# Moving the first group's value products beside its own attention in a fused decoder layer

## The chip, the core and the metric

The kernel runs on one core of one Trainium2 chip. The metric is the device time of one execution, in microseconds (us). Five engines work side by side, each through its own instructions in order: TensorE (PE in the profile, its weight loads PEld), VectorE (DVE), ScalarE (ACT), GpSimd (POOL) and SyncE (SP), which here only issues DMA transfers. They wait for each other through semaphores. "Clock" below is the TensorE clock that the chip granted, 1.00 being full speed.

## The reference

The input x has 16 batches of 128 tokens with 512 features; a context of the same shape goes with it. One decoder layer is followed by one gated cross-attention layer, both with 16 heads of 32 features, all in 32-bit floats:

```python
qkv = layernorm(x, ln1_s, ln1_b) @ w_qkv + b_qkv            # A: self-attention
x = x + attention(q, k, v, ltor_mask) @ w_ao + b_ao
x = x + attention(layernorm(x, ln2) @ w_q + b_q, ctx @ w_kv + b_kv, cross_mask) @ w_co + b_co   # B
x = x + gelu(layernorm(x, ln3) @ w1 + b1) @ w2 + b2         # C: MLP
a = layernorm(ctx, gamma, beta)                             # D: gated cross-attention
out = x + tanh(gate) * attention(x @ Wq.T, a @ Wk.T, a @ Wv.T) @ Wo.T
```

## The kernel before

The 16 batches are four groups of four; a group has 512 tokens. The stages are A0 to A3 (self-attention of groups 0 to 3), B0 to B3 (cross-attention), C (the MLP) and D0 to D3. Activations that are multiplied by weights lie with features on the 128 partitions, as four chunks of 128 features by 512 tokens.

**Block products.** The q, k and v products of stage A are not computed as 16 plain matmuls each. `block_product` (L376) cuts the weight and the activation into 2 x 2 quarters and makes seven products of quarters, numbered 1 to 7, instead of eight, with sums of quarters made beforehand: `left_blocks` (L357) makes four sums for a weight (s3, a21 in place, s2, s4), once for all groups; `right_blocks` (L367) makes four for a group's normalized activation (t1, t2, b12 in place, t4), in tiles that all groups share (`tokens_at`). Products 1, 6 and 7 add up one after the other in PSUM bank mm0 and are copied out by ACT between; 5 and 3 add up in mm1; 2 and 4 rotate through the two pt banks. DVE adds the pieces together: these adds are put into a queue (`afterwards`) and are issued by `due()` at the start of the next step, so DVE stands behind the products of the step before.

**Attention.** `attend` (L567) goes through the sections in steps k, 16 to a section, four to a batch. A unit is four heads of one batch. At the first step of a batch PE makes its scores into the four sc banks. Each unit then goes through scaling (DVE), mask addition (POOL), minimum (DVE, one step later), four exponentials (ACT), reciprocal (DVE, two steps later) and normalization (POOL), a 32 x 32 transpose (DVE, three steps later) and a trip through DRAM, which leaves the probabilities turned (away, pT; issued by SP). Ten steps after its batch's first step come the mix with v (av, PE), and two steps on the output projection (mo, PE).

**What runs beside it.** While section i's attention runs, `jobs()` of section i + 1 hands out that section's block products by step (`BLOCKS`, L432), and `prepare(p)` of section i + 2 loads and normalizes: layer norm of one batch at p = 0, 2, 4, 6 with its transpose and its send to DRAM, the four receive DMAs at p = 9, and at p = 12 to 15 one chunk each of the turned activation (T_A, also lnT), written by ACT. Within a step the order is: scores, `due()`, the jobs, output projection, mix, `prepare`, then the units' work. All instructions are kept in program order on each engine, SP's DMA issues too.

**The start.** Section A0 has nothing before it. `begin` (L670) normalizes group 0, turns it on PE, and makes the q weight's sums on POOL. Then `attend` (L574 to L581) runs 16 steps without attention: all 21 products of A0 by `BLOCKS`, the other eight weight sums on DVE (L730), group 1's `prepare`, and the small jobs (L196 to L205): the output weight of A, the mask, gate and bias rows, the key masks, group 2's x, and the gated k weight (`gated_weight`, L1126), which is loaded in 16 small pieces and turned on DVE. With `at_start` set, the layer norm's last step is done by DVE and not by ACT. Profiles give L49 for nearly all instructions, since one helper records them; they are told apart by the names of the tiles.

Of the kernel before, what the change touches and what calls it, by code (L numbers as in the profile page):

```python
# [10 lines left out]
F32 = mybir.dt.float32  # L11
U8 = mybir.dt.uint8
AF = mybir.ActivationFunctionType
# [3 lines left out]
P = 128  # L17
# [4 lines left out]
H = 512  # L22
# [3 lines left out]
GB = 4  # L26
# [26 lines left out]
def decoder_then_gated_cross_attention(ctx: ExitStack, tc: tile.TileContext, a: dict, out: bass.AP):  # L53
    nc = InOrder(tc)
# [26 lines left out]
    def due():  # L81

        left = [do for queue in (late["dve"], late["act"]) for do in queue]
        for queue in late.values():
            queue.clear()
        for do in left:
            do()


    def load_weight(ap, r0, c0, name):  # L90

        t = wpool.tile([P, KC, H], F32, tag="w", name=name)
        nc.sync.dma_start(out=t, in_=ap[r0 : r0 + H, c0 : c0 + H].rearrange("(k p) n -> p k n", p=P))
        return t
# [14 lines left out]
    def load_batch(g, b):  # L109
        nc.sync.dma_start(out=x[g][:, b, :], in_=a["x"][g * GB + b])  # L110
# [24 lines left out]
    def load_vectors(n, engine=nc.sync, parts=slice(None)):  # L135
        row = 0
        for i, (_, ap) in enumerate(vectors[n]):
            size = ap.shape[0] // P
            if i in range(len(vectors[n]))[parts]:
                engine.dma_start(out=rows_of[n][row : row + size, :], in_=ap.rearrange("(c p) -> c p", p=P))  # L140
            row += size

    def turn_vectors(n):
        rows, (cols, _) = rows_of[n], columns[vectors[n][0][0]]
        nrow = rows.shape[0]
        tv = ps("mm", f"tv{n}")
        nc.tensor.transpose(tv[:, 0:nrow], rows, ident[0:nrow, 0:nrow])
        nc.vector.tensor_copy(cols, tv[:, 0:nrow])
# [6 lines left out]
    w = {}  # L155
# [31 lines left out]
    def key_masks():  # L187
# [5 lines left out]
        nc.tensor.transpose(tm[:, 0:NB], mrow, ident[0:NB, 0:NB])  # L193
        nc.vector.tensor_copy(mcol, tm[:, 0:NB])

    def small_jobs():  # L196
        def load_output_weight():
            w["so"] = load_weight(a["L0_xattn_w_ao"], 0, 0, "w_ao")
# [237 lines left out]
    )  # L436

    def blocks_plan(products):
        out = {}
        for jobs, steps_ in zip(products, BLOCKS):  # L440
# [126 lines left out]
    def attend(sections, ready, others, after=None):  # L567

        if not ready:
            sections[0].begin(sections[1])  # L574
            jobs = sections[0].jobs()
            for p in range(NS):
                due()
                for job in jobs.get(p, ()):
                    job()
                if p + 1 < NS:  # L580
                    sections[1].prepare(p + 1)  # L581
        at_start[0] = False
        units, batches = [], []
        projected = deque()

        def step(k, bt=None, jobs=(), ahead=None, last=True):

            m = k % GB
            pair = k - 5
            if pair % 2 and 0 <= pair < len(units):  # L590
                receive_pair(*units[pair])
            if m == 0 and bt is not None:
                scores(bt)
            due()
# [12 lines left out]
            if ahead is not None:  # L607
                ahead.prepare(k % NS)
            if 0 <= k - 3 < len(units):
                turn_unit(*units[k - 3])  # L610
            if 0 <= k - 2 < len(units):
                norm_unit(*units[k - 2])
            if 0 <= k - 1 < len(units):
                least_unit(*units[k - 1])
                exp_unit(*units[k - 1])
            if bt is not None:
                for j in SCALED[m]:
                    scale_unit(bt, j)
                bt.sec.add_mask(by_head(bt.s[m]), bt.b)

        k = 0
        for i, sec in enumerate(sections):
            last = i + 1 == len(sections)
            jobs = others() if last else sections[i + 1].jobs()
            ahead = sections[i + 2] if i + 2 < len(sections) else after if i + 2 == len(sections) else None
            for b in range(GB):
                bt = Batch(sec, b)
                batches.append(bt)
                for m in range(GB):
                    units.append((bt, m))  # L630
# [15 lines left out]
    def add_row(g, row_, b):  # L646
        nc.gpsimd.tensor_tensor(x[g][:, b, :], x[g][:, b, :], row_, ALU.add)


    class SelfAttention(Section):  # L650
# [19 lines left out]
        def begin(self, following):  # L670
# [26 lines left out]
            following.prepare(0)  # L697
            transposed_out(self.lnT, tp, "ln1_s", "ln1_b")

        weight_sums = []  # L700
        v_bias = "b_qkv", 2 * KC

        def jobs(self):
            g, n, lnT = self.g, self.name, self.lnT
            if g == 0:

                gw_k = work.tile([P, GB, H], F32, tag="v", name="gw_k", bufs=2)
            qkv_tiles(self)
            sides, todo = right_blocks(lnT, self.tokens_at)
            sums = [lambda o=o: nc.gpsimd.tensor_tensor(*o) for o in todo], [0, 0, 1, 2]  # L710
            if g == 0:
                sums = [], []
                for o in todo:
                    nc.vector.tensor_tensor(*o)
            v = self.v
            products = [
                block_product(halves(self.q), self.weights[0], sides, False, f"q_{n}", ("b_qkv", 0)),
                block_product(halves(self.k), self.weights[1], sides, False, f"k_{n}", ("b_qkv", KC)),
                block_product(
                    [[v[:, 2 * j : 2 * j + 2, i * HF : (i + 1) * HF] for j in range(2)] for i in range(2)],  # L720
                    self.weights[2], sides, True, f"v_{n}",
                ),
            ]
            more = ()
            if g == 0:
# [12 lines left out]
        def scale_mask(self, s, sc, b):  # L738
            nc.vector.tensor_tensor(s, sc, bcast_rows(ms1), ALU.mult)
# [622 lines left out]
```

## Time and profile before

| | |
|---|---|
| Median of three runs | 1205.36 us (1204.84 to 1208.3) |
| Profiled execution, its own time | 1208.67 us |
| Span in its trace | 1206.7 us |
| Mean clock over the span | 0.993 |
| PE, DVE, ACT, POOL busy | 1169.3, 749.4, 580.8, 594.2 us |
| First scores of A0, of A1, of A2 begin | 56.62, 112.79, 173.92 us |
| 0 to 20 us: PE, DVE, ACT, POOL busy | 11.75, 15.40, 3.85, 11.33 us |
| 20 to 40 us | 18.46, 19.39, 4.53, 11.27 us |
| 40 to 60 us | 17.51, 9.40, 4.72, 3.99 us |
| 56.6 to 112.8 us (A0's stage), clock 0.94 | 51.22, 44.15, 38.57, 44.58 us |
| 112.8 to 173.9 us (A1's stage), clock 1.00 | 60.31, 51.27, 41.87, 48.20 us |

All times in the trace count from the start of the span. A row of the timeline gives the start, the busy time, the engine, the operation with its output and inputs, the number of instructions merged, and in brackets how long the engine stood idle ahead of it and what released it. A row of the groups gives the count, the busy time in all and the mean of one in ns, then the idle time ahead. A row by stretch gives PE, PEld, DVE, ACT and POOL busy time, the granted clock, the DMA engines' busy share and GB/s. In the row of busy digits each digit is a fortieth of the span, in tenths. PE's matmuls overlap, so their busy times may add up to more than the time from start to start.

### The profile page before, as it was taken

Reading aid. Unit: us, or ns where it says so; the run is one execution under the profiler, and the core shown is the slowest. Engines: PE = TensorE matmul, PEld = TensorE weight load, DVE = VectorE, ACT = ScalarE, POOL = GpSimd, SP = SyncE. Lnnn points to the kernel's source line nnn. Section 1 sums busy time; section 2 is a strip of 40 time slices with the busy share of each in tenths; the row PEclk is TensorE's granted clock in tenths of the full one; section 3 lists DMA queues with packets and bytes.
Section 4 is the critical chain, followed back from the end, with each engine's and each line's share of the span. In section 5 each row is a group of like instructions: output and inputs, shape, how many; then the busy total and the mean of one; then the engine's idle time right before and its main releaser. Section 6 shows DMA issues by size and latency. Waiting matters only on the chain. (4 is left out here: it accounts for less than half of the span.)

```text
span 1206.7 us, 20209 instructions
## 1 busy us (share of the span) xinstructions
PE 1169.3 (97%) x6707; PEld 774.5 (64%) x6707; DVE 749.4 (62%) x1452; ACT 580.8 (48%) x2038; POOL 594.2 (49%) x547
## 2 busy tenths in 40 slices
PE   7889999999999999997999999999999999999997
PEld 5777777644444444444788888888888754444443
DVE  8687979776877767865754634542532255648673
ACT  2266767665655656663232222222222246868552
POOL 4397868585757656575223524433441233324231
PEclk9989999999999999999999999999999999999999
DMA  6756878897988978697695484585457638676575
GB/s 209 195 166 168 224 205 210 234 263 210 206 223 194 235 210 225 190 269 219 213 324 194 160 283 150 190 278 193 149 205 241 175 98 221 175 198 190 159 227 182
DMA packets 317983, 249.18 MB, mean 206 GB/s; under 512 B 82932, under 2 KB 278200, under 8 KB 313016
## 3 DMA queue, kind: packets, MB, share of 16 engines
q1 hardware_dynamic: 317840, 247.89, 70.4%
q8 instruction: 53, 0.87, 0.3%
q14 instruction: 50, 0.41, 0.1%
q10 hardware_dynamic: 40, 0.01, 0.0%
HBM read 158.70 MB, written 89.13 MB: 205 GB/s over the span
## 5 line engine op out<-in xcount | busy, mean ns | idle before, releaser
L49 ACT ACTIVATE s_B<-s_B,mn_B 128x128 f32<-128x128 f32 x256 | 99.5, 390 | 80.3 <-issue 60.6
L49 POOL TENSOR_TENSOR s_D<-s_D,sum_D 128x512 f32<-128x512 f32 x64 | 66.5, 1039 | 143.9 <-DVE sum_D L49 138.0
L49 DVE TENSOR_TENSOR h<-h,h 128x512 f32<-128x512 f32 x80 | 54.9, 687 | 119.5 <-PE h L49 119.1
L49 ACT ACTIVATE s_A<-s_A,mn_A 128x128 f32<-128x128 f32 x256 | 99.5, 393 | 57.3 <-issue 33.3
L49 ACT ACTIVATE s_D<-s_D,mn_D 128x128 f32<-128x128 f32 x256 | 99.4, 390 | 42.2 <-issue 34.7
L49 ACT ACTIVATE h<-h 128x512 f32<-128x512 f32 x64 | 40.3, 630 | 159.0 <-DVE h L49 154.8
L49 POOL TENSOR_TENSOR s_B<-s_B,sum_B 128x512 f32<-128x512 f32 x64 | 66.9, 1045 | 63.7 <-DVE sum_B L49 56.0
L49 POOL TENSOR_TENSOR s_A<-s_A,sum_A 128x512 f32<-128x512 f32 x64 | 66.5, 1039 | 51.1 <-DVE sum_A L49 50.0
L49 POOL TENSOR_TENSOR s_B<-s_B,mask 128x512 f32<-128x512 f32 x64 | 81.6, 1275 | 5.2 <-DVE s_B L49 3.1
L49 POOL TENSOR_TENSOR s_A<-s_A,ma 128x512 f32<-128x512 f32 x64 | 81.6, 1276 | 3.3 <-DVE s_A L49 1.6
L49 POOL TENSOR_TENSOR sh<-h 128x512 f32<-128x512 f32 x32 | 41.5, 1296 | 53.1 <-ACT h L49 43.3
L49 PE MATMUL h<-T_C,w 128*128 128x256 f32 x256 | 62.7, 389 | 1.2 <-DVE h L49 1.2
L49 POOL TENSOR_TENSOR rstd_aD<-rstd_aD,mhalf 128x1 f32<-128x1 f32 x12 | 6.6, 548 | 115.2 <-DVE rstd_aD L49 101.8
L49 PE MATMUL h<-sx,t 128*128 128x256 f32 x256 | 60.7, 380 | 1.1 <-POOL sx L49 1.1
L49 PE MATMUL h<-T_C,t 128*128 128x256 f32 x256 | 60.6, 379 | 0.1
L49 PE MATMUL mo_D<-w_go,mT_D 128*128 128x512 f32 x128 | 57.9, 601 | 2.9 <-ACT mT_D L49 2.9
L49 PE MATMUL o<-w,h 128*128 128x256 f32 x256 | 60.5, 379 | 0.0
L49 PE MATMUL o<-t,h 128*128 128x256 f32 x256 | 60.5, 379 | 0.0
L49 PE MATMUL o<-t,sh 128*128 128x256 f32 x256 | 60.5, 379 | 0.0
L49 PE MATMUL mo_B<-w_co,mT_B 128*128 128x512 f32 x128 | 59.0, 604 | 1.3 <-ACT mT_B L49 1.3
L49 PE MATMUL mm_q_D<-T_D,w_gq 128*128 128x512 f32 x128 | 59.4, 613 | 0.0
L49 PE MATMUL mo_A<-w_ao,mT_A 128*128 128x512 f32 x128 | 59.2, 605 | 0.0
(220 smaller groups left out, 2752.9 us busy)
## 6 DMA issues: line engine op xcount, KB each, us to landing
t<-kept SPq DMA_DIRECT2D x24, 1024.0 KB, 9.0
away_A<-s_A SPq DMA_DIRECT2D x64, 256.0 KB, 2.4
pT_A<-away_A SPq DMA_DIRECT2D x128, 128.0 KB, 2.9
away_B<-s_B SPq DMA_DIRECT2D x64, 256.0 KB, 4.5
pT_B<-away_B SPq DMA_DIRECT2D x128, 128.0 KB, 3.3
away_D<-s_D SPq DMA_DIRECT2D x64, 256.0 KB, 3.1
pT_D<-away_D SPq DMA_DIRECT2D x128, 128.0 KB, 2.8
w<-in_L_xattn_w_dram SPq DMA_DIRECT2D x24, 512.0 KB, 5.3
```

Of the source, the lines that this page charges most:

```text
L49: return lambda *args, **kw: self.tc.keep_in_program_order(call(*args, **kw))
```

## The change

The 16 steps ahead of the first attention become seven, in a method `start`. They hold the q and k products of group 0 (`FIRST_BLOCKS`), the eight k and v weight sums, now on POOL, the small loads and mask terms, two of group 2's x loads, and `prepare` of group 1 in a closer order. A0's attention takes in group 0's seven v products in its first four steps, group 1's 21 products in the other twelve (`SECOND_BLOCKS`), group 1's activation sums in steps 2 to 5 and its last two chunks in step 0. The output weight, the bias rows, the gate's tanh, the key masks, the rest of group 2's x and all of group 3's, the bias row that is added to group 0's x, and the gated k weight are moved into the steps of A0's attention too. The gated k weight takes a buffer of the tag `enc` where it had one of the tag `v`. The diff, with the move of one inner function left out:

```diff
     def small_jobs():
         return (
-            [load_output_weight, load_small, lambda: load_vectors(1, parts=slice(0, 4)),
-             lambda: load_vectors(1, parts=slice(4, None)), lambda: mask_terms(ms1, ma1),
-             lambda: nc.scalar.activation(gate, gate, AF.Tanh), lambda: turn_vectors(1), key_masks],
-            [5, 4, 6, 7, 8, 10, 10, 11],
-        ), ([lambda b=b: load_batch(2, b) for b in range(GB)], [9, 11, 13, 15])
+            [load_output_weight, lambda: load_vectors(1, parts=slice(0, 4)),
+             lambda: load_vectors(1, parts=slice(4, None)), lambda: nc.scalar.activation(gate, gate, AF.Tanh),
+             lambda: turn_vectors(1), key_masks],
+            [1, 2, 3, 8, 9, 13],
+        ), ([lambda b=b: load_batch(2, b) for b in range(2, GB)], [1, 3]), (
+            [lambda b=b: load_batch(3, b) for b in range(GB)], [5, 7, 9, 11]
+        )
...
+    FIRST_BLOCKS = (
+        {0: (1, 2), 1: (6, 5), 2: (7, 4), 3: (3,)},
+        {3: (1,), 4: (6, 2), 5: (7, 5), 6: (4, 3)},
+    )
+    SECOND_BLOCKS = (
+        {4: (1, 2), 5: (6, 5), 6: (7, 4), 8: (3,)},
+        {7: (1, 2), 8: (6,), 9: (7, 5), 10: (4,), 11: (3,)},
+        {12: (1,), 13: (6, 2), 14: (7, 5), 15: (4, 3)},
+    )
...
         if not ready:
-            sections[0].begin(sections[1])
-            jobs = sections[0].jobs()
-            for p in range(NS):
-                due()
-                for job in jobs.get(p, ()):
-                    job()
-                if p + 1 < NS:
-                    sections[1].prepare(p + 1)
+            sections[0].start(sections[1])
...
+        def start(self, following):
+            self.begin(following)
+            _, todo = self.tiles()
+            for o in todo:
+                nc.vector.tensor_tensor(*o)
+            key_sums, value_sums = self.weight_sums[1:]
+            prepare = [lambda p=p: following.prepare(p) for p in (2, 4, 6, 9, 12, 13)], [0, 1, 2, 4, 6, 6]
+            jobs = plan(
+                *blocks_plan(self.products(), FIRST_BLOCKS), prepare,
+                ([lambda o=o: nc.gpsimd.tensor_tensor(*o) for o in key_sums], [0, 1, 2, 3]),
+                ([lambda o=o: nc.gpsimd.tensor_tensor(*o) for o in value_sums], [4, 5, 6, 6]),
+                ([load_small, lambda: mask_terms(ms1, ma1)], [2, 5]),
+                ([lambda b=b: load_batch(2, b) for b in range(2)], [3, 5]),
+            )
+            for p in range(max(jobs) + 1):
+                due()
+                for job in jobs[p]:
+                    job()
+            due()
...
-        def jobs(self):
-            g, n, lnT = self.g, self.name, self.lnT
-            if g == 0:
-                gw_k = work.tile([P, GB, H], F32, tag="v", name="gw_k", bufs=2)
+        def tiles(self):
             qkv_tiles(self)
-            sides, todo = right_blocks(lnT, self.tokens_at)
-            sums = [lambda o=o: nc.gpsimd.tensor_tensor(*o) for o in todo], [0, 0, 1, 2]
...
-            more = ()
-            if g == 0:
-                others = [o for todo in self.weight_sums[1:] for o in todo]
-                rows = [lambda b=b: add_row(0, bo_row, b) for b in range(GB)]
-                more = (
-                    *small_jobs(), *gated_weight("k", gw_k, range(4, 12), range(12, 16)), (rows, range(8, 12)),
-                    ([lambda o=o: nc.vector.tensor_tensor(*o) for o in others], [1, 2, 3, 3, 4, 5, 6, 7]),
-                )
-            elif g == 1:
-                more = [([lambda b=b: load_batch(3, b) for b in range(GB)], [1, 3, 5, 7])]
-            elif g == 2:
-                more = gated_weight("v", act_tile("gw_v", "enc"))
-            return plan(sums, *blocks_plan(products), *more)
+        def jobs(self):
+            g = self.g
+            _, todo = self.tiles()
+            sums = [lambda o=o: nc.gpsimd.tensor_tensor(*o) for o in todo]
+            if g > 1:
+                more = gated_weight("v", act_tile("gw_v", "enc")) if g == 2 else ()
+                return plan((sums, [0, 0, 1, 2]), *blocks_plan(self.products(), BLOCKS), *more)
+            first = decoder[0]
+            return plan(
+                *blocks_plan(first.products()[2:], FIRST_BLOCKS), (sums, [2, 3, 4, 5]),
+                *blocks_plan(self.products(), SECOND_BLOCKS), *small_jobs(),
+                ([lambda p=p: self.prepare(p) for p in (14, 15)], [0, 0]),
+                ([lambda b=b: add_row(0, bo_row, b) for b in range(GB)], range(8, 12)),
+                *gated_weight("k", act_tile("gw_k", "enc"), range(4, 12), range(9, 16, 2)),
+            )
```

More of the change, by code (lines that the diff above doesn't have):

```diff
@@ L194, in key_masks, with load_output_weight @@
         nc.vector.tensor_copy(mcol, tm[:, 0:NB])
+    def load_output_weight():
+        w["so"] = load_weight(a["L0_xattn_w_ao"], 0, 0, "w_ao")
     def small_jobs():
-        def load_output_weight():
-            w["so"] = load_weight(a["L0_xattn_w_ao"], 0, 0, "w_ao")
         return (
-            [load_output_weight, load_small, lambda: load_vectors(1, parts=slice(0, 4)),
-             lambda: load_vectors(1, parts=slice(4, None)), lambda: mask_terms(ms1, ma1),
-             lambda: nc.scalar.activation(gate, gate, AF.Tanh), lambda: turn_vectors(1), key_masks],
-            [5, 4, 6, 7, 8, 10, 10, 11],
-        ), ([lambda b=b: load_batch(2, b) for b in range(GB)], [9, 11, 13, 15])
+            [load_output_weight, lambda: load_vectors(1, parts=slice(0, 4)),
[5 more added lines that the diff above has]
+        )
     def squares(ap):
@@ L436, in decoder_then_gated_cross_attention, with blocks_plan @@
     )
-    def blocks_plan(products):
+    FIRST_BLOCKS = (
[3 more added lines that the diff above has]
+    SECOND_BLOCKS = (
[3 rows of a table added]
+    )
+    def blocks_plan(products, blocks):
         out = {}
-        for jobs, steps_ in zip(products, BLOCKS):
+        for jobs, steps_ in zip(products, blocks):
             for step, ns in steps_.items():
@@ L698, in begin, with products @@
             transposed_out(self.lnT, tp, "ln1_s", "ln1_b")
+        def start(self, following):
[17 more added lines that the diff above has]
+            due()
         weight_sums = []
         v_bias = "b_qkv", 2 * KC
-        def jobs(self):
-            g, n, lnT = self.g, self.name, self.lnT
-            if g == 0:
-                gw_k = work.tile([P, GB, H], F32, tag="v", name="gw_k", bufs=2)
+        def tiles(self):
             qkv_tiles(self)
-            sides, todo = right_blocks(lnT, self.tokens_at)
-            sums = [lambda o=o: nc.gpsimd.tensor_tensor(*o) for o in todo], [0, 0, 1, 2]
-            if g == 0:
[L712 to L716, printed above, removed]
+            self.sides, todo = right_blocks(self.lnT, self.tokens_at)
+            return self.sides, todo
+        def products(self):
+            n, v, sides = self.name, self.v, self.sides
+            return [
                 block_product(halves(self.q), self.weights[0], sides, False, f"q_{n}", ("b_qkv", 0)),
@@ L723, in jobs @@
             ]
-            more = ()
-            if g == 0:
-                others = [o for todo in self.weight_sums[1:] for o in todo]
-                rows = [lambda b=b: add_row(0, bo_row, b) for b in range(GB)]
-                more = (
-                    *small_jobs(), *gated_weight("k", gw_k, range(4, 12), range(12, 16)), (rows, range(8, 12)),
-                    ([lambda o=o: nc.vector.tensor_tensor(*o) for o in others], [1, 2, 3, 3, 4, 5, 6, 7]),
-                )
-            elif g == 1:
-                more = [([lambda b=b: load_batch(3, b) for b in range(GB)], [1, 3, 5, 7])]
-            elif g == 2:
-                more = gated_weight("v", act_tile("gw_v", "enc"))
-            return plan(sums, *blocks_plan(products), *more)
+        def jobs(self):
[13 more added lines that the diff above has]
+            )
         def scale_mask(self, s, sc, b):
```

## The prediction

> **What bounds the kernel now.** I read the busy totals first, then TensorE (PE) in order of time, then busy time by stretch, then the groups.
>
> ```profile
> PE 1169.3 (97%) x6707; PEld 774.5 (64%) x6707; DVE 749.4 (62%) x1452; ACT 580.8 (48%) x2038; POOL 594.2 (49%) x547
> PE   7889999999999999997999999999999999999997
> ```
>
> PE is the bound, and the digits under 9 at the left are where the change works: the first three slices of 30.2 us. PE's timeline, line = start, busy, what, and the wait ahead of it:
>
> ```profile
> 12.65 5.30 PE L49 MATMUL mm_q_A<-T_A,w_sq 128*128 128x256 f32 x16 [0.23 <-ACT T_A L49]
> 17.79 1.89 PE L49 MATMUL mm_q_A<-sums_A,sums 128*128 128x256 f32 x8
> ...
> 24.17 1.89 PE L49 MATMUL mm_k_A<-T_A,w_sk 128*128 128x256 f32 x8
> 25.89 1.89 PE L49 MATMUL mm_q_A<-sums_A,w_sq 128*128 128x256 f32 x8
> ...
> 56.62 1.17 PE L49 MATMUL sc_A<-k_A,q_A 32*128 32x128 f32 x32
> ...
> 80.57 1.88 PE L49 MATMUL sc_A<-k_A,q_A 32*128 32x128 f32 x26 [2.32 <-DVE s_A L49]
> 83.31 3.78 PE L49 MATMUL mm_k_A<-T_A,sums 128*128 128x256 f32 x8 [0.86 <-ACT k_A L49]
> ...
> 112.79 1.17 PE L49 MATMUL sc_A<-k_A,q_A 32*128 32x128 f32 x32
> ...
> 173.92 1.17 PE L49 MATMUL sc_A<-k_A,q_A 32*128 32x128 f32 x32
> ```
>
> The scores (sc_A) mark the stages. Group 0's 21 block products run alone from 12.65 to 56.62; A0's attention, with group 1's 21 products, to 112.79; A1's to 173.92. One product (x8) takes 1.725 us from start to start (24.17 to 25.89). Likewise a batch's scores take 1.10, its mix (av) 1.05, its output projection (mo) 3.54.
>
> A1's stage: 21 x 1.725 + 4 x (1.10 + 1.05 + 3.54) = 59.0 of its 61.13 us; 0.78 of the rest is one wait on k, 1.3 is switching from one kind of matmul to another. That is a PE-bound stage. A0's stage holds 36.2 + 4.4 + 2 x 1.05 + 3.54 = 46.3 of PE work in 56.17: 9.9 lost. The start holds 36.2 in 43.97: 7.8 lost. The 17.7 us are all that this change can reach. Where A0 loses is seen by stretch (PE, PEld, DVE, ACT, POOL busy, granted clock, DMA share):
>
> ```profile
> 78.00:80.00 2.00, 0.25 (x6) 0.06 (x3) 1.93 (x7) 0.08 (x1) 1.52 (x3) 1.00 0.49 137
> 82.00:84.00 2.00, 1.14 (x8) 0.76 (x4) 1.97 (x5) 2.00 (x8) 1.49 (x2) 0.50 0.40 115
> 84.00:86.00 2.00, 2.00 (x6) 1.58 (x5) 1.47 (x4) 1.12 (x7) 2.00 (x3) 0.50 0.89 251
> 60.00:80.00 20.00, 17.23 (x109) 14.23 (x107) 18.25 (x39) 12.89 (x52) 18.99 (x19) 1.00 0.46 132
> ```
>
> In the first eight steps VectorE (DVE) and GpSimd (POOL) are full (18.25 and 18.99 of 20), so PE waits 2.32 us for a score bank; then the clock is half from about 80.6 to 87.2, which costs 6.6 / 2 = 3.3.
>
> **The change, part by part.**
>
> Start. 14 products (q, k) remain ahead of the scores. The first two still take 5.14 instead of 3.45 (until 17.79), because the in-place sums and lnT are no earlier: +1.7. The 0.93 waits on ACT's copies of q and k, the 1.70 wait on the late bias rows and the 0.8 on DVE go: between two products of bank mm0 there is now always one of another bank, and the rows' transpose is gone from here. New is a wait that v used to cover: scores need the last k add. After v's last product the DVE add began 0.2 us after PE's end and took 0.69; with its signal back, 1.1. Scores at 12.65 + 14 x 1.725 + 1.7 + 1.1 = 39.6, with 0.3 for a late k sum 39.9: 16.7 earlier.
>
> The eight k and v weight sums go from DVE to POOL. The rows:
>
> ```profile
> L49 DVE TENSOR_TENSOR sums<-w_sv 128x512 f32<-128x512 f32 x2 | 2.4, 1223 | 0.0
> L49 POOL TENSOR_TENSOR sums<-w_sq 128x512 f32<-128x512 f32 x2 | 2.5, 1260 | 0.1
> L49 POOL TENSOR_TENSOR x<-x,bao_row 128x512 f32<-128x512 f32 x11 | 14.7, 1349 | 3.3 <-DVE ln_A L49 3.3
> ```
>
> POOL's four q sums took 1.26, 1.33, 1.26, 1.62, mean 1.37, so the eight take 10.9; DVE sheds 8.8 in the same eight (1.23, 1.23, 0.69, 0.69, 1.22, 0.69, 1.22, 1.79). With four row adds (1.3) and rstd powers (0.55) POOL has 18.3 us in a start of about 24. Its queue, followed in order from 15.4, ends the third k sum, which product k6 needs, at 27.6; PE gets to k6 at 28.2. The Trainium skill, "GPSIMD Engine Reference", section "Performance versus the Vector engine", speaks against this move: POOL takes 1.96 times as long as DVE for such an add. By that, a sum costs 8.8 / 8 x 1.96 = 2.15, s2 ends 3 x 0.78 later, at 29.9, and PE waits 1.7. The q row is the same shape on the same engine beside the same DVE load; I take it, and keep 1.7 for the range.
>
> Group 1's layer norm is squeezed into seven steps: its last send leaves near 28, the four receive DMAs follow behind load_small (3 issues, 2.1 us on SP) and two x loads (0.4 each). The weight and gk loads that filled the DMA then (share 0.96 to 1.10 from 46 to 52; 6.7 us from receive to first use) are moved past it. Landing takes between 2.9 (the pT row's median) and 6.7: lnT at 34.5 to 38.5, before the scores either way, so nothing is charged. If it were over 44, ACT's copy of v1 would stand behind it and PE with it.
>
> A0's stage. PE now has 28 products: 28 x 1.725 = 48.3, + 4.4 + 2.1 + 3.54 = 58.3, + 1.3 for switches. By batches of four steps it is 13.2, 14.9, 12.5, 17.7. The other side: POOL has 1.27 (mask) + 1.04 (norm) a step, four group 1 sums in steps 2 to 5 (1.27), a row add and rstd every second step until 7, and four bo_row adds moved here in steps 8 to 11 (1.27): added up, 28.9 by the end of step 7 and 43.3 by step 11, against PE's 28.1 and 40.6. The next batch's scores need only the mask of three steps before (step 9's, at 36.1), so POOL and DVE have some 3 us to spare. Before, 24.0 us lay between scores 0 and 2 with two sums and one to two adds fewer; +2.5 for POOL gives 26.5 against PE's 28.1 and switches. So I charge no scores wait and no half clock.
>
> The clock is where the second rule of the skill stands against me. "TensorE: Matmul & The Clock Gate", section "Why this matters for your kernels", asks only that PE not idle for over about 3 us. This trace shows a drop right after 2.32. By the rule the wait is not the cause, the drop may come again, and 3.3 has to be given back. By the row it goes with the wait. I side with the row, because no drop stands in A1's to A3's stages, where waits are 0.8 at most, and keep 3.3 for the range.
>
> One wait I do charge. The turn of the second set of vectors goes to step 8: its copy on DVE waits for a PE transpose that now stands behind k6 and q3. Behind that copy queue turn, reciprocal, minimum and scale (0.70 + 0.15 + 0.67 + 0.68 = 2.2) and only then q3's add (0.69), which frees bank mm1 for k5 in step 9, with one product (1.73) between on PE: 2.9 - 1.7 + 0.2 = 1.4. The k add that PE waits 0.78 for now is freed by k3's move to step 11. In step 13 the key masks do the same to DVE, but with v7 before v5 nothing waits. 0.6 for small waits (nearest row 0.78; nought to 2).
>
> SP in this stage: 16 gk issues (0.5 us, 8 us in all), nine vector rows (0.3), the 1 MB w_ao (0.5) in step 1, six x loads. A1's stage now has 16 such gated loads in steps 0 to 7 and no wait on pT; receives are due two steps (7 us) before the mix. w_ao is due at step 12, 40 us on. Charged nothing; a late pT would be a wait at step 10, of 0 to 4 (6.7 less 2.9).
>
> Sum: 39.9 + 58.3 + 1.3 + 1.4 + 0.6 = 101.5 for A1's first scores, against 112.79: **11.3 us less**. After that no work changes but x3's loads (earlier) and the gated v weight's buffer, which is free as A1's stage begins. The profiled execution, span 1206.7, took 1208.67, so it would take 1197.4; the median of the runs lies 3.3 lower, so 1205.36 - 11.3 = **1194**.
>
> **Rivals.** *One clock drop.* PE waits once for scores (batch 2 or 3), as at 80.57: 2.3 + 3.3 = 5.6 back, 5.7 gained, 1199.7. For it: DVE and POOL are full in just those steps and both get more. Against: PE gets four to five us more as well.
>
> *Nothing moves*: two such waits, 11.2, 1205.
>
> *Slower*: the softmax chain bounds the whole stage. PE outruns it and waits at the scores of batches 1, 2 and 3, each 2.3 and each with its half clock: 16.8, so 1205.4 + 5.5 = 1211. It decides from the third wait on, that is, once a unit of the chain costs over (112.8 - 39.9) / 16 = 4.55 us. Before, a unit cost 24.0 / 8 = 3.0; for it speaks that DVE waits in order for adds from PE, and PE for DVE, so lags can feed each other.
>
> **How the numbers follow.** Likeliest 0.66, at 1194, its own range 1190 to 1198; one drop 0.14; nothing moves 0.06; slower 0.14. The low end: if no time at all were lost but what start and switches cost, A1's scores stand at 12.65 + 24.2 + 1.7 + 58.3 = 96.9, 16 less, 1189. The high end reaches past the one drop with the 1.7 of a slow sum and part of the lost-gain case, 1204; left out are the slower case and the rest, under 0.2. Faster by over 0.3% (3.6 us, about what a measurement of this kernel can tell from no change): 0.66 + 0.14 = 0.80; within 0.3%: 0.06; slower: 0.14.
>
> **What would show it.** Right: first scores near 40, with a wait of about 1; A1's first scores at 100 to 103; granted clock 1.00 from 60 to 100; stages A1 and later as long as now (61.1). The sum fails at the start if k6 waits on POOL or if the first chunks of lnT come after 44; it fails in A0 if sc_A waits on DVE with the clock at 0.5 behind it. It would be wrong outright if A0's stage took over 73 us, or a later stage over 62.

## The result and the profile after

The changed kernel takes **1201.73 us** in the median of eight runs (1194.9 to 1202.3), against 1207.64 for the kernel before in eight runs beside them (1204.32 to 1209.92; the table further up has the first three of these). The ratio is **0.9943, interval 0.9921 to 0.9964**: some 7 us faster, 4.3 to 9.5 (the two medians lie 5.9 apart). Its profiled execution took 1202.3, with a span of 1200.0 and a mean clock of 0.996.

The busy totals and the row of busy digits, to be laid beside those of before:

```profile
PE 1165.7 (97%) x6707; PEld 772.2 (64%) x6707; DVE 745.7 (62%) x1444; ACT 581.6 (48%) x2038; POOL 603.8 (50%) x555
PE   7989999999999999998999999999999999999997
```

POOL has eight instructions more and DVE eight fewer, which are the eight weight sums. The second slice is now 9, but the third is 8: a loss is left between 60 and 90 us. PE in order of time (start, busy, what, the wait ahead of it) shows where:

```profile
12.49 5.78 PE L49 MATMUL mm_q_A<-T_A,w_sq 128*128 128x256 f32 x16 [0.23 <-ACT T_A L49]
18.11 1.89 PE L49 MATMUL mm_q_A<-sums_A,sums 128*128 128x256 f32 x8
...
27.72 1.97 PE L49 MATMUL mm_q_A<-T_A,sums 128*128 128x256 f32 x8 [0.80 <-POOL rstd_A L49]
...
39.97 1.17 PE L49 MATMUL sc_A<-k_A,q_A 32*128 32x128 f32 x32
...
65.04 3.38 PE L49 MATMUL mm_q_A<-T_A,sums 128*128 128x256 f32 x8 [3.40 <-ACT q_A L49]
68.25 1.89 PE L49 MATMUL mm_q_A<-sums_A,w_sq 128*128 128x256 f32 x8
...
86.00 1.99 PE L49 MATMUL mm_k_A<-T_A,sums 128*128 128x256 f32 x8 [1.06 <-DVE k_A L49]
...
106.43 1.17 PE L49 MATMUL sc_A<-k_A,q_A 32*128 32x128 f32 x32
...
123.35 3.70 PE L49 MATMUL mo_A<-w_ao,mT_A 128*128 128x512 f32 x8 [1.12 <-ACT mT_A L49]
...
169.48 1.17 PE L49 MATMUL sc_A<-k_A,q_A 32*128 32x128 f32 x32
```

| | before | after | difference |
|---|---|---|---|
| A0's first scores | 56.62 | 39.97 | 16.65 earlier |
| A1's first scores | 112.79 | 106.43 | 6.36 earlier |
| A2's first scores | 173.92 | 169.48 | 4.44 earlier |
| end of the span | 1206.7 | 1200.0 | 6.7 earlier |

The first scores come 16.65 us earlier, but 12.1 of that (7 x 1.725) is only v's work moved behind them: the start lost 7.8 before and loses 3.2 now, 4.6 less. A0's stage takes 66.46 where the prediction had 61.6. Of this 58.3 is PE's work, so it loses 8.1 where it lost 9.9, only 1.8 less. Together that is the 6.36 at A1's scores, of the 11.3 predicted. A1's stage takes 63.05, not 61.1, and 1.9 more are gone. (Late in the span some 2 us come back, from a stretch near 960 to 1000 us at a clock of 0.96 in the execution before and of 1.00 in this one; a second execution of the changed kernel had 0.96 there too, so this is not the change's doing.)

The 4.9 us that A0's stage takes over the predicted 61.6 lie in one place. By stretch (PE, PEld, DVE, ACT and POOL busy, clock, DMA):

```profile
62.00:64.00 2.00, 0.00 (x0) 0.00 (x0) 2.00 (x4) 0.65 (x1) 1.31 (x2) 1.00 0.00 0
64.00:66.00 2.00, 0.96 (x2) 0.84 (x3) 2.00 (x4) 2.00 (x10) 1.79 (x2) 0.62 0.51 133
66.00:68.00 2.00, 2.00 (x6) 1.61 (x5) 1.93 (x7) 0.43 (x3) 2.00 (x3) 0.52 0.96 275
```

PE is idle for 3.40 us ahead of product q7, and then has half the clock, so that this product takes 3.21 (65.04 to 68.25) and not 1.73. PE waits for ACT's copy of q6. Followed backwards, DVE's, ACT's and POOL's rows of those microseconds give the chain:

```profile
59.89 3.43 DVE L49 SCALAR_TENSOR_TENSOR off_A<-mv_A,rstd_A 128x1 f32<-128x1 f32 x1 [0.56 <-POOL rstd_A L49]
63.24 0.70 DVE L49 STREAM_TRANSPOSE s_A<-s_A 128x512 f32<-128x512 f32 x1
```

```profile
63.35 0.81 ACT L49 ACTIVATE ln_A<-x,off_A,rstd_A 128x512 f32<-128x512 f32 x1 [3.54 <-DVE off_A L49]
64.08 0.82 ACT L49 ACTIVATE q_A<-mm_q_A,vcols 128x256 f32<-128x256 f32 x2
```

```profile
59.29 0.57 POOL L49 TENSOR_TENSOR rstd_A<-rstd_A,mhalf 128x1 f32<-128x1 f32 x1
59.81 1.06 POOL L49 TENSOR_TENSOR s_A<-s_A,sum_A 128x512 f32<-128x512 f32 x1
60.81 1.28 POOL L49 TENSOR_TENSOR s_A<-s_A,ma 128x512 f32<-128x512 f32 x1
62.03 1.28 POOL L49 TENSOR_TENSOR sums_A<-sums_A,T_A 128x512 f32<-128x512 f32 x1
64.14 1.04 POOL L49 TENSOR_TENSOR s_A<-s_A,sum_A 128x512 f32<-128x512 f32 x1 [0.84 <-DVE sum_A L49]
```

`off` is one number per partition, minus the mean times rstd, made by DVE for a layer norm that ACT finishes (L240). In the trace of before it took between 0.12 and 1.22, and in A0's stage at most 0.99:

```profile
66.05 0.99 DVE L49 SCALAR_TENSOR_TENSOR off_A<-mv_A,rstd_A 128x1 f32<-128x1 f32 x1 [0.29 <-POOL rstd_A L49]
```

Here it takes 3.43, over the very time in which POOL runs three instructions without a gap, the last of them an activation sum that the change put into step 5; both engines' rows end together. ACT's norm waits for `off`, the copy of q6 stands behind the norm on ACT, and PE stands behind the copy. In A1's stage another `off` of 2.22, at 119.98, stands ahead of the wait on mT of 1.12 in the same way. That `off` is itself the cause, and not a bystander, is tested below.

### The profile page after: what moved, and what is told of

Read it like the earlier page. It is cut to its first block, busy times and chain, and to the rows that moved or that the text cites. A ratio compares the mean times of both kernels' runs of the same rounds, so it can differ in the third digit from the quotient of the medians.

```text
span 1200.0 us, 20209 instructions
## 1 busy us (share of the span) xinstructions
PE 1165.7 (97%) x6707; PEld 772.2 (64%) x6707; DVE 745.7 (62%) x1444; ACT 581.6 (48%) x2038; POOL 603.8 (50%) x555
## 5 line engine op out<-in xcount | busy, mean ns | idle before, releaser
L49 PE MATMUL h<-T_C,w 128*128 128x256 f32 x256 | 61.1, 381 | 1.2 <-DVE h L49 1.2
L49 PE MATMUL mm_v_D<-w_gv,T_a 128*128 128x512 f32 x128 | 59.9, 616 | 0.0
```

What stands on the lines that cost most here:

```text
L49: return lambda *args, **kw: self.tc.keep_in_program_order(call(*args, **kw))
```

## The experiments

Diffs are against the changed kernel unless said otherwise. Theories are named in capitals, and the expectations use these names.

**`off` with one tensor input.** HELD says that DVE's instruction with two tensor inputs is held while POOL runs; LOAD says that POOL simply has too much to do in these steps, so that whatever waits for it waits as long. The same value can be made by an instruction with one tensor input, rstd as its scalar. The changed kernel ran beside it once more.

```diff
-            nc.vector.scalar_tensor_tensor(off, mv[:, 0:1], -1.0, rstd, ALU.mult, ALU.mult)
+            nc.vector.tensor_scalar(off, mv[:, 0:1], rstd, -1.0, ALU.mult, ALU.mult)
```

> The changed kernel as it is, for comparison on this chip. Both theories: time 5 to 7 us under the kernel before (ratio 0.994 to 0.996); A0's first scores at 40, one wait of about 3.4 us on ACT's q copy near 62 to 65 with half clock behind it, A1's first scores near 106.4, A2's near 169.5.

> The layer norm's 128x1 offset is computed by a tensor_scalar with rstd as its scalar, so the instruction has one tensor input instead of two. Theory HELD (DVE's two-input off is held while POOL runs without a gap, and with it ACT's normalization, the q copy behind it and PE): every off takes 0.15 to 0.3 us, PE's 3.4 us wait and the half clock behind it (1.5) go, A1's first scores at 101 to 102 instead of 106.4, A1's stage 61.1 instead of 63.1; in all 5 to 7 us under the changed kernel. Rival LOAD (POOL has too much to do in steps 2 to 5, and whatever waits for it waits just as long): off is short, but the wait moves to the reciprocal or the minimum behind it; A1's first scores stay at 105 to 107.

The changed kernel again: 1201.3, ratio 0.9943 (0.9929 to 0.9957). The `off` of 3.43 and the wait of 3.38 were there again; the clock stayed at 1.00 this time, and A0's stage took 65.04. With one input: **1196.49**, ratio **0.9901 (0.9884 to 0.9917)**. Its DVE and PE at the same place:

```profile
62.38 0.21 DVE L49 TENSOR_SCALAR off_A<-mv_A,rstd_A 128x1 f32<-128x1 f32 x1 [0.94 <-POOL rstd_A L49]
```

```profile
28.49 3.23 PE L49 MATMUL mm_q_A<-T_A,sums 128*128 128x256 f32 x8 [2.48 <-POOL rstd_A L49]
...
64.31 1.96 PE L49 MATMUL mm_q_A<-T_A,sums 128*128 128x256 f32 x8 [0.21 <-ACT q_A L49]
...
104.89 1.17 PE L49 MATMUL sc_A<-k_A,q_A 32*128 32x128 f32 x32
...
166.06 1.17 PE L49 MATMUL sc_A<-k_A,q_A 32*128 32x128 f32 x32
```

The wait of 3.4 is 0.21, and A1's stage is back at 61.17 without any wait on mT. LOAD falls: POOL's and DVE's work is the same, and the wait does not come back elsewhere. What shows on the other side is the start, where q3 waited 2.48, at half clock after it, instead of 0.80; the edit touches nothing there (the end of the next section comes back to it). A0's first scores are therefore 2.5 later (42.43), and its stage, at 62.46, is 4.0 shorter. So HELD's number for A1's first scores, 101 to 102, was missed by the start's doing, and 4.8 us by the medians is a little under its 5 to 7. All the `off` rows of this trace lie between 0.17 and 0.21.

The Trainium skill, "SBUF — State Buffer", section "Who interferes with whom", says that a DVE instruction with two inputs in SBUF contends with a POOL instruction that reads SBUF, and one with a single input outside the two-port modes doesn't. The pair of kernels agrees: 3.43 with two inputs and 0.21 with one.

**The bias rows' turn ahead of the products.** ROWS says that the wait of 1.06 on k's add comes from the turn of the second vectors in step 9, whose DVE copy waits for a PE transpose behind that step's products. If the transpose is issued ahead of them, the wait goes; COVER says that it is due to the thin cover between k products and stays. Then this edit and the last one together.

```diff
-             lambda: turn_vectors(1), key_masks],
-            [1, 2, 3, 8, 9, 13],
+             key_masks],
+            [1, 2, 3, 8, 13],
...
+                ([lambda: turn_vectors(1)], [9]),
                 *blocks_plan(first.products()[2:], FIRST_BLOCKS), (sums, [2, 3, 4, 5]),
```

> The transpose of the late bias rows is put ahead of step 9's products on PE instead of behind them; nothing else. Theory ROWS (DVE's copy of these rows waits for PE's products and keeps the k add, and so bank mm1, late): DVE's idle time from 76 to 82 shrinks by about 3.5 us, PE's 1.06 us wait on the k add before k3 goes, 1.1 us under the changed kernel, the 3.4 us wait near 62 stays. Rival COVER (the k add is late for POOL's masks anyway): the wait stays at 0.8 to 1.1 and the time is that of the changed kernel.

> Both edits. HELD and ROWS together: A1's first scores at 100 to 101, 6 to 8 us under the changed kernel, 12 to 14 under the kernel before. LOAD and COVER: not more than 2 us under the changed kernel.

Rows first alone: 1201.01, ratio 0.9934 (0.9913 to 0.9956); the 1.06 is gone, the wait of 3.39 and its half clock remain, and A0's stage takes 65.58. The mechanism of ROWS is right and COVER falls, but a microsecond is below what the time can tell. Both: **1195.9, ratio 0.9901 (0.9886 to 0.9917)**. PE of the two together:

```profile
28.21 2.73 PE L49 MATMUL mm_q_A<-T_A,sums 128*128 128x256 f32 x8 [2.22 <-POOL rstd_A L49]
...
42.15 1.17 PE L49 MATMUL sc_A<-k_A,q_A 32*128 32x128 f32 x32
...
76.45 0.26 PE L49 MATMUL tv<-ident,vrows 48*128 48x48 f32 x1
...
103.47 1.17 PE L49 MATMUL sc_A<-k_A,q_A 32*128 32x128 f32 x32
```

A0's stage takes 61.32 and A1's 61.14, close to the prediction's sums (61.6 and 61.1), 5 us under the changed kernel's A0. A1's first scores were expected at 100 to 101 and stand at 103.47, for the start was late here too (42.15). By the medians this is 5.4 us under the changed kernel, where 6 to 8 were expected, and 12.4 under the kernel before.

**v in the start.** The change does two things: it squeezes the start and it sets v beside the attention. TWO PARTS says that each earns its share; COVER BY V says that the small jobs, moved into A0's attention, need v's products there. Here the start is as close as in the changed kernel, but makes v's seven products too, in steps 7 to 10:

```diff
-                *blocks_plan(self.products(), FIRST_BLOCKS), prepare,
+                *blocks_plan(self.products(), FIRST_BLOCKS + ({7: (1, 2), 8: (6, 5), 9: (7, 4), 10: (3,)},)), prepare,
...
-                *blocks_plan(first.products()[2:], FIRST_BLOCKS), (sums, [2, 3, 4, 5]),
-                *blocks_plan(self.products(), SECOND_BLOCKS), *small_jobs(),
-                ([lambda p=p: self.prepare(p) for p in (14, 15)], [0, 0]),
+                (sums, [0, 0, 1, 2]), *blocks_plan(self.products(), BLOCKS), *small_jobs(),
```

> The squeezed start alone: group 0's seven v products go back ahead of the first scores (steps 7 to 10 of the start), group 1's 21 products run over all of A0's attention as in the kernel before, the rest stays as changed. Theory TWO PARTS (the start's lost time and A0's lost time are recovered separately): first scores at 51 to 52, that is 5 earlier than before; A0's stage 55 to 57 as before, since off is held and PE waits there; A1's first scores at 107 to 108, 0 to 2 over the changed kernel. Rival COVER BY V (all that the change gains comes from putting v beside attention): first scores not before 54, A1's first scores at 110 or later, 4 or more over the changed kernel.

Measured: 1210.32 (22 runs) against 1207.05 (35 runs), ratio **1.003 (1.0016 to 1.0043), slower than before**. PE of this kernel:

```profile
52.88 1.17 PE L49 MATMUL sc_A<-k_A,q_A 32*128 32x128 f32 x32
...
76.83 1.12 PE L49 MATMUL sc_A<-k_A,q_A 32*128 32x128 f32 x26 [2.32 <-DVE s_A L49]
79.57 3.78 PE L49 MATMUL mm_k_A<-T_A,sums 128*128 128x256 f32 x8 [1.62 <-ACT k_A L49]
...
107.27 3.75 PE L49 MATMUL mm_v_A<-w_sv,sums_A 128*128 128x256 f32 x8 [4.09 <-DVE k_A L49]
116.47 1.17 PE L49 MATMUL sc_A<-k_A,q_A 32*128 32x128 f32 x32
```

The squeezed start brings the first scores 3.7 earlier (a microsecond later than TWO PARTS had them), but A0's stage then takes 63.59 instead of 56.17. The scores wait of 2.32 is the one of before. The 4.09 is new. DVE's row ahead of it says why:

```profile
103.22 0.17 DVE L49 COPY mcol<-tm 128x16 f32<-128x16 f32 x1 [2.00 <-PE tm L49]
```

This is the key masks' copy, which waits for PE in step 13; k's add queues behind it on DVE, and v5 behind that. The changed kernel has the masks in the same step and no such wait, because it makes the last k product in step 11: in step 13 of `BLOCKS` that product stands directly ahead of the masks (101.13), in `SECOND_BLOCKS` v's do. So TWO PARTS falls in its second half: in this form the squeezing alone brings nothing, and the gain hangs on v's products standing beside the attention, where they also cover the small jobs. COVER BY V is the nearer of the two, though neither had all the numbers. That squeezing is worth nothing wherever the small jobs stand is not shown. Without the 4.09 and the half clock behind it (some 2.8), and with the 0.78 that the kernel before waits at this place, A1's scores would stand near 110.4. This is an estimate from these rows: 2.4 earlier than before, and still 4 later than in the changed kernel. No run has this kernel with the masks elsewhere. The profiled execution, at 1215.69, is also one of the slowest of the 22, so the usual loss may be smaller than the rows show.

**`off` in the kernel before.** EVERYWHERE says that the one-input form is worth its 5 us in any version; HELD says that it pays only where an `off` meets a run of POOL's. The one-line edit on the kernel before:

> The kernel before with the layer norm's offset from one tensor input, nothing else. Theory HELD: the longest off falls from 1.0 to 0.2; as POOL's runs were shorter there (offs of 0.15 to 1.0 in A0's and A1's stages), the gain is 0 to 2 us, and PE's 2.3 us wait for scores shrinks but may stay. Rival EVERYWHERE (the offset's form is worth about 5 us whatever the plan, in stages B and C too): 4 to 6 us under the kernel before.

Measured: 1207.35, ratio **1.0002 (0.999 to 1.0014)**. The scores wait of 2.32 and its half clock are untouched. EVERYWHERE falls; the hold became a cost through the change, which put POOL's sums and `off` into the same steps with little slack behind them.

**The weight sums back on DVE.** RULE is the prediction's doubt about this move, that POOL's slower sums cost the start time; HELD IN THE START looks to DVE's own rows, which are slow because POOL runs beside them.

```diff
-                ([lambda o=o: nc.gpsimd.tensor_tensor(*o) for o in key_sums], [0, 1, 2, 3]),
-                ([lambda o=o: nc.gpsimd.tensor_tensor(*o) for o in value_sums], [4, 5, 6, 6]),
+                ([lambda o=o: nc.vector.tensor_tensor(*o) for o in key_sums], [0, 1, 2, 3]),
+                ([lambda o=o: nc.vector.tensor_tensor(*o) for o in value_sums], [4, 5, 6, 6]),
```

> The eight k and v weight sums go back to DVE, in the same steps; all else as changed. Theory HELD IN THE START (POOL's sums hold DVE's 128x512 normalization, 1.48 instead of 0.53): normalizations fall to 0.5 to 0.9 and the sums cost DVE 0.7 to 1.2 each, so the first scores stay at 39 to 42, and the time is within 2 us of the changed kernel. Rival RULE (POOL is 1.96 times as slow and is what makes PE wait before q3): PE's wait before q3 goes, first scores at 38 to 39, 1 to 2 us under the changed kernel.

Measured: 1198.97, ratio 0.9929 (0.9913 to 0.9945), which overlaps the changed kernel's interval. First scores at 39.93, q3's wait 0.94: as with the sums on POOL, so RULE falls. DVE's rows beside POOL are indeed slow, but they are not all that makes q3 wait. On DVE such a sum took 0.68 with POOL idle and 1.23 beside POOL, against POOL's 1.27. The layer norm's subtraction on DVE shows the same split: 1.49 in the changed kernel's start beside POOL, 0.55 here.

```profile
24.06 0.55 DVE L49 TENSOR_SCALAR ln_A<-x,mv_A,rstd_A 128x512 f32<-128x512 f32 x1 [0.44 <-POOL rstd_A L49]
...
26.25 0.68 DVE L49 TENSOR_TENSOR sums<-w_sk 128x512 f32<-128x512 f32 x1
...
59.85 0.99 DVE L49 SCALAR_TENSOR_TENSOR off_A<-mv_A,rstd_A 128x1 f32<-128x1 f32 x1 [0.56 <-POOL rstd_A L49]
```

The last row was the surprise: in A0, where nothing differs, `off` took 0.99 and q7 waited 0.96. The same kernel was therefore profiled a second time:

> The kernel weights_on_dve once more. If the length of the hold is a matter of tens of nanoseconds and not of where the weight sums are made, the off of step 5 may take 3.4 this time, with PE's wait of 3.4 behind it; if moving the weight sums takes the hold away for good, it takes 1.0 again.

```profile
60.24 3.43 DVE L49 SCALAR_TENSOR_TENSOR off_A<-mv_A,rstd_A 128x1 f32<-128x1 f32 x1 [0.56 <-POOL rstd_A L49]
```

PE's wait behind it was 3.38, at half clock after it (1201.28 us in this one run). The length of the hold differs between executions of **one kernel**, though POOL's sequence is the same. That is one likely source of the changed kernel's own spread (1194.9 to 1202.3); single runs were not profiled often enough to show it.

**The start's norms on ACT.** HELD IN THE START and DRIFT (the q3 wait of 2.2 to 2.5 is chance) were set against each other on top of the two edits together:

```diff
             self.begin(following)
+            at_start[0] = False
```

> Both edits (offset from one input, bias rows' transpose first), and in the start the last step of group 1's normalization goes to ACT for batches 1 to 3, as it does later. Theory HELD IN THE START: DVE sheds 1.3 us a step, PE's wait of 0.8 to 2.5 us before q3 goes with the half clock that followed the longer ones; first scores at 38 to 40, A1's first scores at 99 to 101; 1 to 3 us under the kernel with both edits. Rival DRIFT (that wait comes from the q weight's late landing, 0.8 us from one execution to the next, and not from DVE's load): the wait stays at 0.8 to 2.5 and the time is that of both edits.

Measured: 1195.77, ratio 0.99 (0.9883 to 0.9917); first scores 39.64, A1's at 100.98. The q3 wait is gone, so DRIFT falls, but PE waits 2.06 for ACT's copy of q at 22.18 instead. In the profiled executions the first scores came 2.5 earlier than with the two edits alone, and yet the medians agree, where HELD IN THE START had 1 to 3 us. The lead still stands at B's first scores (288.26 against 290.71) and is gone at C's first product (547.19 against 546.70). Between them, from 520 to 547 us, two of stage B's mixes wait for the DMA that brings pT: 2.04 and 2.85 here, 1.36 and 2.09 there, and the half clock behind them lasts 6.83 here and 3.41 there. The kernel before has such waits too (1.97 and 0.77 at this place). Whether they swallow the lead every time, one profile of each can't tell.

**POOL's run longer and shorter.** In its first form HELD said that DVE is held until POOL's queue is empty. Its rival, ACT, looks for the wait in ACT's queue and expects 3.4 in both runs. Longer: the last activation sum is made twice, to the same values.

```diff
-                (sums, [2, 3, 4, 5]),
+                (sums + sums[3:], [2, 3, 4, 5, 5]),
```

> The changed kernel with its two-input off, and the last of group 1's activation sums (t4) made twice in step 5, so that POOL's unbroken run behind which off stands is one instruction of 1.27 us longer. Theory HELD, in the form that weights_on_dve leaves (the held off gets through either at the first boundary between two POOL instructions, after about 1.0 us, or only when POOL's queue is empty): the off of step 5 takes 4.7 us, or else 1.0; PE's wait before q7 is 4.7, or else 1.0. Rival ACT (the wait comes from ACT's own queue and off is only a bystander): off and wait stay at 3.4.

Shorter: the sum of step 5 is moved out of it.

```diff
-                (sums, [2, 3, 4, 5]),
+                (sums, [2, 2, 3, 4]),
```

> The changed kernel with group 1's activation sums in steps 2, 2, 3, 4 instead of 2, 3, 4, 5, so that nothing of them stands in POOL's queue in step 5. HELD: the off of step 5 is held for a normalization and a mask, 2.2 us, or else 1.0, and PE's wait before q7 is 2.2 at most. ACT: 3.4.

Longer, one run of 1204.15; its DVE and POOL:

```profile
60.23 3.43 DVE L49 SCALAR_TENSOR_TENSOR off_A<-mv_A,rstd_A 128x1 f32<-128x1 f32 x1 [0.57 <-POOL rstd_A L49]
```

```profile
62.36 2.64 POOL L49 TENSOR_TENSOR sums_A<-sums_A,T_A 128x512 f32<-128x512 f32 x2
64.95 1.04 POOL L49 TENSOR_TENSOR s_A<-s_A,sum_A 128x512 f32<-128x512 f32 x1
```

POOL ran on without a gap to beyond 65, yet `off` ended at 63.66, between the two sums. It was let in at the third end of a POOL instruction, not at the end of the run: HELD in that form falls. PE's wait was 3.40, as in the changed kernel, which is the number that ACT had. Shorter, one run of 1200.92: `off` took 0.99, as hoped, but it began only at 61.86, as POOL's rstd stood behind the moved sum, and q7 waited 2.21 all the same: an instruction of POOL's ahead of rstd costs as well as one behind it. HELD had 2.2 at most and ACT 3.4, so each theory has the number of one run. Since the length of the hold differs between executions of one kernel, these two single runs settle no more than that it doesn't last to the end of POOL's run. They do not decide against ACT. The one-input kernel does: it has ACT's queue as it was and a wait of 0.21.

**All three together.** The one-input `off`, the rows first and the sums on DVE:

> Off from one input, bias rows' transpose first, and the eight weight sums on DVE: the candidate for the best. PE's wait before q3 at 0.9 to 1.0 without half clock, first scores at 40, A0's stage 61.3, A1's first scores at 101; 0 to 2 us under the kernel with both edits, and a ratio of 0.988 to 0.990 to the kernel before.

Measured: 1195.76, ratio 0.9896 (0.9874 to 0.9917). A0's stage takes 61.32 again. The start was not as expected: q3 waited 2.18 with half clock behind it and not 0.9 to 1.0, so the first scores stand at 42.08 and A1's at 103.40. This kernel, the two edits together, and the one with the norms on ACT can't be told apart; they are the best versions found, some 12 us under the kernel before and 5 to 6 under the changed one.

## Why the prediction was right, and where it was not

The direction was right, and the time, 1201.7 where 1194 was predicted, lies inside the range of 1189 to 1204; the size is some 7 us of 11.3. Of the mechanism, the start's half came as forecast (4.6 us recovered). A0's half came to 1.8 us where the sum had 6.6. It was there to be had, as the two edits together show: at 61.32 A0's stage loses 3.0 and recovers 6.9. The likeliest case's own range, 1190 to 1198, was missed, and the result lies nearer to the rival "one clock drop" (1199.7). Of the signs named for being right only the first scores near 40 came, and those without their wait of about 1; A1's first scores stand at 106.43 and not at 100 to 103, the clock was not 1.00 throughout, and A1's stage took 63.05. That last is over the 62 which the prediction had named, for a later stage, as the sign of being wrong outright. The time held in spite of it, because the range was 15 us wide.

*The start.* 39.9 predicted, 39.97 measured, but this closeness is luck: misses that cancel. The first two products took 5.62 and not 5.14, q3 waited 0.80 for DVE's adds, which stood behind POOL's rstd, and going from one kind of product to another cost some 0.4; the sum had none of this. In exchange the k sum was not late at k6 (0.3), and the 1.1 for the last k add did not come at all. DVE began that add after the scores had begun at 39.97:

```profile
40.08 0.69 DVE L49 TENSOR_TENSOR k_A<-mm_k_A,k_A 128x512 f32<-128x512 f32 x1 [1.04 <-PE mm_k_A L49]
```

The last product, k3, makes the quarter of k with the tokens of batches 2 and 3 (c12 in `block_product`), which the first batch's scores don't read.

*The weight sums.* POOL's row was the right price: 1.27 each, the prediction having taken 1.37 and not the rule's 2.15. The rule's ratio isn't far off with POOL idle beside DVE (1.27 to 0.68 is 1.87); it misled because DVE's price was the one that varied.

*lnT.* Predicted to land at 34.5 to 38.5; ACT had the wait for it until 39.3, and it cost PE nothing.

*A0's stage.* **"So I charge no scores wait and no half clock" is the step that failed.** Its first half held, since no score waited for DVE. But another wait stood there: 3.40 ahead of q7, plus about 1.5 for the clock, which is the 4.9 between 61.6 and 66.46. The sum counted the work of POOL and DVE, each instruction at its usual length, and asked whether the totals fit. It had no term for a DVE instruction on one number a partition that can last three POOL instructions, nor for ACT, whose queue passed the delay on to PE. Without that hold the stage takes 62.46, and with the bias rows' wait gone too 61.32. So the PE count was close but not exact: besides the 58.3 of work and the waits, some 2.2 to 2.4 goes into switching between kinds of matmul, and not 1.3. The sum of 61.6 comes near because the small waits were charged too high.

*The rival.* "One clock drop" gave 1199.7, with 5.7 gained from a wait of 2.3 and a half clock of 3.3. The size is close to what happened (3.4 + 1.5), by another engine's wait.

*The bias rows.* The kind of wait was right and its size close (1.4 predicted, 1.06 measured), but the turn was put in step 8, where the tanh is; it is in step 9, so the wait came at k3 in step 11 and not at k5.

*The clock.* The rule that the prediction quotes, under which PE may stand idle for about 3 us, is not a safe bound here: the profiles have half clock after waits of 2.18, 2.22, 2.32 and 2.48. But the row with which the prediction sided is no threshold either. There is no half clock after 2.06, 2.21 and, in one execution of the changed kernel, 3.38. And a wait of 1.42 or 1.43 ahead of D's first scores, which all fourteen profiles have, was followed by half clock within 2 us in nine of them, the kernel before among them, and not in the other five, the changed kernel's first profile among them. By stretch (as above), in the kernel before and in the changed one from the end of that wait:

```profile
978.45:981.87 3.42, 3.42 (x5) 1.35 (x4) 3.42 (x8) 1.65 (x8) 0.01 (x1) 0.50 0.51 153
```

```profile
972.18:977.10 4.92, 4.92 (x35) 2.78 (x36) 4.62 (x9) 1.69 (x9) 0.50 (x2) 1.00 0.38 115
```

So the length of one wait does not decide, and one row could not forecast it.

*A1's stage.* 61.1 was right as a count, but 63.05 came; an `off` of 2.22 stood ahead of the wait there, as in A0. With the one-input form the stage takes 61.17. *Slower* and *nothing moves* did not come about.

*The wait ahead of q3.* In the start q3 waited 2.18 to 2.48 in the three profiles with the one-input form (norms on DVE), and 0.80 to 1.73 in the eight of the squeezed start with the two-input form. The start makes no `off`, so the form has no part in it. The traces show two chains that meet. q3 begins when DVE's adds, behind the norms, free its bank, and that chain starts with the q weight's landing: with the sums on POOL q3 began 18.07 to 18.17 us after POOL's first sum in all eight profiles, and with them on DVE 17.60 to 17.69 in all three. The wait is what PE is early by. It had begun the product before q3 at 24.06 to 24.12 in the three, and at 24.68 to 25.70 in the eight. Why it was early in just these three is open; chance is not ruled out. Behind q3 the first scores of A0 followed after 12.25 or 12.26 us, and after 13.94 in the three, which had half clock.

Still open: why `off` is let in at the first, second or third boundary.

## What to carry to other kernels

Before work is moved to POOL, look at what DVE does beside it, above all at small two-input instructions on whose result another engine's in-order queue depends; write them with one tensor input and a scalar where that can be done. When an engine's totals fit but little slack lies behind one of its results, follow that result through every queue it passes, ACT's too, to PE. And when a start is squeezed, ask first which products will cover the small jobs that are pushed out of it.

## What the runs showed of the hardware

- A 128x1 DVE instruction with two tensor inputs lasted 0.12 to 0.15 at the shortest, and 0.99, 2.2 or 3.43 where POOL ran without a gap in A0's and A1's stages: until the first, second or third end of a POOL instruction. With one tensor input it took 0.17 to 0.22 throughout, in five kernels. The page quoted above lets the loser block until the other instruction has finished; here it was up to three of them, and it differed between two executions of one kernel.
- A 128x512 subtraction and multiplication on DVE took 0.53 to 0.55 with POOL idle and 1.49 beside it, with one tensor input as well; an addition took 0.68 and 1.23.
- Between 20 us and the last products every drop to half clock lasted 3.41 us or twice that, 6.83, in all fourteen profiles (for example 64.50 to 67.91 in the changed kernel and 80.75 to 87.57 in the kernel before). By that a drop costs at most 1.7 or 3.4 us, an estimate. The same wait had a drop in one execution of a kernel and none in another (3.40 and 3.38 in the changed kernel).
